# A row of scores by two transfers through DRAM instead of four TensorE transposes, and three buffers used in place, in a fused graph network

## The chip, the cores and the metric

The kernel runs on one core of a Trainium2 chip. The metric is the device time of one launch in microseconds (us), from the first to the last instruction, median of the runs. A separate execution is recorded by the hardware profiler: every instruction of the five engines with its start and length, every DMA packet, and the semaphore events between them. TensorE is called PE in the profile (PEld is its weight load), VectorE DVE, ScalarE ACT, GpSimd POOL, SyncE SP.

## The reference

A batch of 128 graphs of 128 nodes with 256 features goes through four layers. Each is `x = layernorm(x + layer(x, adj))`. Layer 0 is a gated graph network, layers 1 to 3 are graph attention (GAT).

```python
# layer 0: three steps
A = (adj != 0)
for i in range(3):
    m = einsum('bnd,de->bne', h, weight[i])
    aggr = einsum('bst,bsd->btd', A, m)
    h = gru_cell(aggr, h, w_ih, w_hh, b_ih, b_hh)
# layers 1 to 3, each with its own W and a
Wh = einsum('bnf,of->bno', x, W)
f_i, f_j = Wh @ a1, Wh @ a2
e = leaky_relu(f_i[:, :, None] + f_j[:, None, :], 0.2)
e = where(adj == 0, very_negative, e)
h_prime = einsum('bij,bjo->bio', softmax(e), Wh)
```

The score of an edge from i to j needs f_i, one number for each partition (node i), and f_j, one number for each column (node j). The numbers f_j come out one per partition, so they have to become a row, and the same row has to stand on all 128 partitions.

## The kernel before

The 128 graphs are 32 groups of G = 4. All arithmetic is in float32. For each group `gru` does the three steps of layer 0 and `gat` the three attention layers. All groups are recorded first as a list of operations, each with its reads, its writes, the engines that could run it and a cost in nanoseconds. The class `Plan` then plays this list through once, at build time, and from it comes the order of instructions on every engine; there is no other scheduler. On the chip each engine runs its own queue strictly in that order, and semaphores enforce the dependencies.

What the planner knows:

- priorities: older groups go first; the last four groups (`LAST = 4`, the tail) get priorities by stage instead, so that their layers run side by side;
- pools of buffers (`pools`): `k2` and `k4` are the SBUF work tiles of 512 and 1024 floats per partition, `bank` and `gate` are the PSUM banks (3 and 5), `fx` takes the unused product of a score, `v` the columns of statistics. `own` keeps some buffers back for the oldest group. An operation starts only if a buffer is free;
- a latency from the end of an operation on one engine to the start of its successor on another, and a margin of 500 ns more where the successor runs on PE:

```python
LATENCY = {"PE": 250, "ACT": 220, "DVE": 200, "POOL": 250, "SP": 4000}
...
when = max([t + (margin + self.LATENCY[e2] if e2 != e else 0 if e == "PE" else 60) for e2, t in o.at.items()],
```

Here `e2` is the engine of the predecessor, which ended at `t`, and `e` that of the operation itself. Transfers are operations of SP of 60 ns, and their landing time is SP's latency. The argument `lag` adds to the latency of one operation. `port=BOTH` tells the planner that DVE and POOL must not run two such operations at the same time.

In `gru`, the adjacency of a group is loaded as integers into a tile of the pool `adj` (L479) and turned into a mask `am` of floats (L483). At the end of layer 0 this mask is turned into zeros and a very negative number (L570), which `gat` adds to the scores. The products of the gates are done with a Strassen scheme: the matmuls on L446, the copies out of PSUM on L506, L510, L513 (ACT) and the additions on L451 (DVE). The input x is loaded a second time for the residual (L569).

In `gat`, per layer and group:

1. L605, DVE: eight products with a sum, four for f_j (h = 1) and then four for f_i (h = 0); the sums go to the tile `f`, the products to `fx`;
2. L614, PE: four transposes of the column f_j, broadcast along the free dimension, against the identity; the bank then has the row f_j on all partitions, for each of the four graphs;
3. L619, DVE: four operations that add the mask to this row, write the result to `e_` and take the maximum over j;
4. L623, ACT: Prelu with f_i as bias; L632 and L636, DVE: the maximum after the leaky ReLU; L640, ACT: Exp with the sum;
5. L647 to L674: transposes of the softmax, its product with x, then the product with W;
6. L680, DVE: division by the sum and addition of x, into `y`; then `layernorm(y, total, xn)`, which writes a new tile `xn`: Square with a sum on ACT (L389), whose squares go into `xn` too and are overwritten later, small steps on DVE and POOL, and the scaling on ACT (L402).

Of the kernel before, what the change touches and what calls it, by code (L numbers as in the profile page):

```python
# [8 lines left out]
F32 = mybir.dt.float32  # L9
I32 = mybir.dt.int32  # L10
AF = mybir.ActivationFunctionType
ALU = mybir.AluOpType
AX = mybir.AxisListType

P = 128
D = 256
KC = D // P
G = 4
# [5 lines left out]
FAR = -5.0 * 2.0 ** 97  # L24
# [23 lines left out]
class Plan:  # L48
# [2 lines left out]

    LATENCY = {"PE": 250, "ACT": 220, "DVE": 200, "POOL": 250, "SP": 4000}

    MARGIN = 500

# [140 lines left out]
def adj_resnorm_kernel(  # L198
# [14 lines left out]
    nc = tc.nc  # L213
    B = x.shape[0]
    NG = B // G
    LAST = 4

    consts = ctx.enter_context(tc.tile_pool(name="consts", bufs=1))
    work = ctx.enter_context(tc.tile_pool(name="work", bufs=1))
    psum = ctx.enter_context(tc.tile_pool(name="psum", bufs=1, space=bass.MemoryType.PSUM))  # L220


    pools = {"gru": 4, "xs": 2, "adj": 2, "am": 5, "k2": 26, "k4": 19, "fx": 2, "f": 3, "mv": 4, "st": 6, "v": 16,
             "gate": 5, "bank": 3}
    own = ({"k2": 8, "k4": 5, "gate": 2, "v": 5, "fx": 0, "st": 0}, {"k2": 4, "k4": 2, "v": 5, "fx": 0, "st": 0})
    floats = {"gru": 0, "k4": 1024, "xs": 1024, "fx": 256, "f": 8, "mv": 8, "st": 6, "v": 4}
    tags = {t: (n, floats.get(t, 512)) for t, n in pools.items()}
    BOTH = ("DVE", "POOL")
    plan = Plan({t: n for t, (n, _) in tags.items()}, own)
    slots = {t: [(psum if t in ("gate", "bank") else work).tile([P, w], I32 if t == "adj" else F32, name=f"{t}{i}")  # L230
                 for i in range(n)] for t, (n, w) in tags.items() if w}

    def T(b):
        if b.at is None:
            width = 1
            for s in b.shape:
                width *= s
            at = slots[b.tag][b.slot][:, 0:width]
            if len(b.shape) == 2:
                at = at.rearrange("p (a b) -> p a b", b=b.shape[-1])  # L240
            elif len(b.shape) == 3:
                at = at.rearrange("p (a b c) -> p a b c", b=b.shape[-2], c=b.shape[-1])
            b.at = at
        return b.at

    def bank():
        return Buf("bank", GN)
# [7 lines left out]
    ident = consts.tile([P, P], F32)  # L255
# [111 lines left out]
            res.append(dst)  # L367
        return res

    def layernorm(y, total, dst, prio):  # L370

        rstd, ve, shift = Buf("v", G), Buf("v", G), Buf("v", G)
        if total is None:
            mv = Buf("mv", G, 2)
            for b in range(G):
                st = Buf("st", 6)
                plan.op({"DVE": 400}, lambda e, b=b, st=st: nc.vector.bn_stats(T(st), T(y)[:, b, :]),
                        reads=[(y, b)], writes=[st], prio=prio)
                plan.op({"DVE": 95}, lambda e, b=b, st=st: nc.vector.bn_aggr(T(mv)[:, b, :], T(st)),
                        reads=[st], writes=[(mv, b)], prio=prio)  # L380
            plan.op({"POOL": 229}, lambda e: nc.gpsimd.tensor_scalar(T(ve), T(mv)[:, :, 1], EPS, None, op0=ALU.add),
                    reads=[(mv, b) for b in range(G)], writes=[ve], prio=prio)
            less, keys = (lambda: T(mv)[:, :, 0]), [(mv, b) for b in range(G)]
        else:
            mean, ss = Buf("v", G), Buf("v", G)
            plan.op({"DVE": 100}, lambda e: nc.vector.tensor_scalar(T(mean), T(total), -1.0 / D, None, op0=ALU.mult),  # L386
                    reads=[(total, b) for b in range(G)], writes=[mean], prio=prio)
            for b in range(G):
                plan.op({"ACT": 490}, lambda e, b=b: nc.scalar.activation(  # L389
                    T(dst)[:, b, :], T(y)[:, b, :], AF.Square, bias=T(mean)[:, b:b + 1], accum_out=T(ss)[:, b:b + 1]),  # L390
                    reads=[(y, b), mean], writes=[(dst, b), (ss, b)], prio=prio)
            plan.op({"POOL": 229}, lambda e: nc.gpsimd.tensor_scalar(  # L392
                T(ve), T(ss), 1.0 / D, EPS, op0=ALU.mult, op1=ALU.add),
                reads=[(ss, b) for b in range(G)], writes=[ve], prio=prio)
            less, keys = (lambda: T(mean)), [mean]
        plan.op({"POOL": 1035}, lambda e: nc.gpsimd.tensor_tensor(T(rstd), T(ve), neghalf, ALU.pow),
                reads=[ve], writes=[rstd], prio=prio)
        plan.op({"DVE": 100}, lambda e: nc.vector.scalar_tensor_tensor(  # L398
            T(shift), less(), -1.0 if total is None else 1.0, T(rstd), op0=ALU.mult, op1=ALU.mult),
            reads=keys + [rstd], writes=[shift], prio=prio)  # L400
        for b in range(G):
            plan.op({"ACT": 500}, lambda e, b=b: nc.scalar.activation(  # L402
                T(dst)[:, b, :], T(y)[:, b, :], AF.Identity, bias=T(shift)[:, b:b + 1], scale=T(rstd)[:, b:b + 1]),
                reads=[(y, b), shift, rstd], writes=[(dst, b)], prio=prio)

    def sums(ms, prio):

# [63 lines left out]

    def gru(g, stage):

        xs, adj_i, am = Buf("xs", G, D), Buf("adj", G, P), Buf("am", G, P)
        prio = stage(g, 0)
        turn = Buf("gru")
        x_g = x[g * G:(g + 1) * G].rearrange("b n d -> n b d")
        plan.op({"SP": 60}, lambda e: nc.sync.dma_start(T(xs), x_g), writes=[xs], prio=prio)
        plan.op({"SP": 60}, lambda e: nc.sync.dma_start(T(adj_i), adj[g * G:(g + 1) * G].rearrange("b s t -> s b t")),  # L479
                writes=[adj_i], prio=prio)  # L480
        if g == 0:
            hidden_weights(prio)
        plan.op({"DVE": 417}, lambda e: nc.vector.tensor_scalar(T(am), T(adj_i), 0, None, op0=ALU.not_equal),  # L483
                reads=[adj_i], writes=[am, turn], prio=prio, port=BOTH)
        hT = transposed(xs, lambda b, c: T(xs)[:, b, c * P:(c + 1) * P], prio)
        h = None
        for i in range(STEPS):
            prio = stage(g, i)
            if g == 0:
                input_weights(i, prio)  # L490
            agg = []
            for c in range(KC):
                b_, a_ = bank(), Buf("k2", GN)
# [23 lines left out]
            nn = strassen([(2, (h_in,)), (2, (a_in,))], halves, prio)  # L517
            hT2 = []
            for c in range(KC):

                o, v, d = rz[c], nn[c], Buf("k2", GN)
# [4 lines left out]
                for gt in range(2):  # L526
                    if c == 0:
                        plan.op({"ACT": 630}, lambda e, gt=gt, o=o, tanh=tanh: tanh(gt, 0, GN, lambda: T(o)[:, gt, :]),
                                reads=[(o, 0), (o, 1)], writes=[(o, 2 + gt)], prio=prio)
                    else:  # L530
                        plan.op({"ACT": 365}, lambda e, gt=gt, tanh=tanh, rz=rz: tanh(
                            gt, 0, H, lambda: T(rz[2])[:, gt * H:(gt + 1) * H]),
                            reads=[rz[2]], writes=[(o, 4 + gt)], prio=prio)
                        plan.op({"ACT": 400}, lambda e, gt=gt, o=o, tanh=tanh: tanh(gt, H, GN, lambda: T(o)[:, gt, H:GN]),
                                reads=[(o, 1), (o, 4 + gt)], writes=[(o, 2 + gt)], prio=prio)
                if c == 1:
                    plan.op({"ACT": 370}, lambda e, v=v, nn=nn: nc.scalar.activation(
                        T(v)[:, 0, 0:H], T(nn[2])[:, 0:H], AF.Identity, bias=bhn[:, 1:2]),
                        reads=[nn[2]], writes=[(v, 0)], prio=prio)
# [26 lines left out]
                hT2.append(d)  # L566
            if last:
                y = Buf("k4", G, D)
                plan.op({"SP": 60}, lambda e: nc.sync.dma_start(T(y), x_g), reads=[agg[0]], writes=[y], prio=prio)  # L569
                plan.op({"DVE": 417}, lambda e: nc.vector.tensor_scalar(  # L570
                    T(am), T(am), 0.0, FAR, op0=ALU.is_equal, op1=ALU.mult), reads=[am], writes=[am], prio=prio, port=BOTH)
            else:
                h2 = [Buf("k2", G, P) for c in range(KC)]
# [14 lines left out]
                        e, T(h2[c]), T(b_).rearrange("p (b d) -> p b d", b=G)), reads=[b_], writes=[h2[c]], prio=prio)  # L588
            if not last:
                h, hT = h2, hT2  # L590
        x1 = Buf("k4", G, D)
        layernorm(y, None, x1, prio)
        return x1, am

    def gat(g, xc, no, stage):

        for l in range(3):
# [9 lines left out]
                        accum_out=T(f)[:, b, h:h + 1]), reads=[(xc, b), (wa, l)], writes=[fx, (f, 2 * b + h)], prio=prio, port=BOTH)  # L607
            e_, pT, y = Buf("k2", G, P), Buf("k2", G, P), Buf("k4", G, D)
            top, nmax, den, rden, total = Buf("v", G), Buf("v", G), Buf("v", G), Buf("v", G), Buf("v", G)
            b_ = bank()  # L610

            def fn(e, b_=b_, f=f):
                for b in range(G):
                    nc.tensor.transpose(T(b_)[:, b * P:(b + 1) * P],  # L614
                                        T(f)[:, b, 1:2].to_broadcast([P, P]), ident)
            plan.op({"PE": 440}, fn, reads=[(f, 2 * b + 1) for b in range(G)], writes=[b_], prio=prio)

            for b in range(G):
                plan.op({"DVE": 215}, lambda e, b_=b_, b=b, e_=e_, top=top: nc.vector.tensor_tensor_reduce(  # L619
                    T(e_)[:, b, :], T(b_)[:, b * P:(b + 1) * P], T(no)[:, b, :], 1.0, 3 * FAR, ALU.add, ALU.max,  # L620
                    T(top)[:, b:b + 1]), reads=[b_, no], writes=[(e_, b), (top, b)], prio=prio)
            for b in range(G):
                plan.op({"ACT": 285}, lambda e, b=b, f=f, e_=e_: nc.scalar.activation(  # L623
                    T(e_)[:, b, :], T(e_)[:, b, :], AF.Prelu, bias=T(f)[:, b, 0:1], alpha=SLOPE),
# [43 lines left out]
            for b0 in range(0, G, 2):  # L668
# [9 lines left out]
                for b in (b0, b0 + 1):  # L678
# [2 lines left out]
                                T(y)[:, b, :], T(b_)[:, (b - b0) * D:(b - b0 + 1) * D], T(rden)[:, b:b + 1],  # L681
                                T(xc)[:, b, :], op0=ALU.mult, op1=ALU.add, accum_out=T(total)[:, b:b + 1]),
                            reads=[b_, rden, (xc, b)], writes=[(y, b), (total, b)], prio=prio)
            xn = Buf("k4", G, D)
            layernorm(y, total, xn, prio)
            xc = xn
        plan.op({"SP": 60}, lambda e: nc.sync.dma_start(out[g * G:(g + 1) * G].rearrange("b n d -> n b d"), T(xc)),
                reads=[(xc, b) for b in range(G)], prio=prio)

# [54 lines left out]
```

## Time and profile before

| what | value |
|---|---|
| time, median of 3 runs | 2719.54 us (2718.88 to 2719.57) |
| span of the profiled execution | 2716.7 us |
| granted TensorE clock | 0.998 |
| L614, transposes of f_j: number, median record | 384, 273 ns |
| L619, row plus mask: number, median record | 384, 284 ns |
| L605, products for f: number, median record | 768, 420 ns |
| L446, matmuls of the gates: number of records, median record | 8064, 379 ns |
| transfer of x for one group, issue to landing | 3.9 us (512 KB) |
| transfer of adj for one group, issue to landing | 2.9 us (256 KB) |
| transfer of the output of one group, issue to landing | 3.0 us (512 KB) |

A record is the time from an instruction's start to its end. Instructions of one engine overlap with the next in its pipeline, so the distance from start to start is shorter. A line of the timeline has the start, the length (of all that it merges), engine, source line, operation, tiles and how many; in brackets stands how long the engine was idle before and which instruction ended that. Busy time of an engine counts the union of its records.

### The profile page before, as it was taken

To read this page: it belongs to the slowest core of one execution; us is meant where nothing else is said; L and a number is where in the kernel's file an instruction comes from. 1 tells how busy PE (TensorE), PEld (TensorE's weight loads), DVE (VectorE), ACT (ScalarE), POOL (GpSimd) and SP (SyncE) were. 2 spreads that over 40 slices of the span, in tenths; PEclk is the share of its full clock that TensorE was granted. 3 is DMA by queue.
4 is the path that set the end of the run, shared out by engine and by line. 5 is a ranking of instruction groups with operands and counts; after the bars stand their busy time and mean duration, and the time that the engine had idled before them with its cause. 6 is when DMAs were issued, how large, how long until landed. Compare 5 with 4: busy or idle time off the path is not lost.

```text
span 2716.7 us, 42471 instructions
## 1 busy us (share of the span) xinstructions
PE 2660.0 (98%) x14536; PEld 2366.2 (87%) x14536; DVE 2026.1 (75%) x6206; ACT 1760.2 (65%) x4632; POOL 593.0 (22%) x738
## 2 busy tenths in 40 slices
PE   7999999999999999999999999999999999999987
PEld 6888889888888888888888888988988888888875
DVE  4677777787787776777876777877777877776696
ACT  3566666666666666666767666666676666665577
POOL 1013222211131222122221222212222312222021
PEclk9999999999999999999999999999999999999999
DMA  3001000000010100001000000100000000000000
GB/s 120 9 20 36 28 5 24 28 28 20 13 33 12 36 20 20 16 20 36 20 28 28 9 28 20 36 20 20 17 20 28 28 24 21 9 9 27 13 1 32
DMA packets 70106, 65.39 MB, mean 24 GB/s; under 512 B 2688, under 2 KB 68224, under 8 KB 69888
## 3 DMA queue, kind: packets, MB, share of 16 engines
q1 hardware_dynamic: 67584, 58.73, 7.1%
q10 hardware_dynamic: 2304, 3.95, 0.4%
q8 instruction: 114, 1.87, 0.3%
q14 instruction: 104, 0.85, 0.1%
HBM read 45.89 MB, written 16.78 MB: 23 GB/s over the span
## 4 chain that ended last, share of the span: by engine, by line
PE 86%; DVE 8%; ACT 3%; issue 1%; DMA 1%; POOL 0%; POOLq 0%; ACTq 0%; SPq 0%; DVEq 0%
PE gate L446 58%; PE bank L674 10%; PE bank L663 6%; PE bank L498 5%; PE bank L579 3%; DVE fx L605 2%; PE bank L647 1%; DVE k L451 1%; PE bank L614 1%; ACT k L402 1%; ACT k L389 1%; DVE k L680 1%; DVE k L286 1%; PE bank L333 1%; DVE k L540 1%
## 5 line engine op out<-in xcount | busy, mean ns | idle before, releaser
L446 PE MATMUL gate<-k,whs 128*128 128x256 f32 x4032 | 1202.2, 380 | 3.0 <-ACT k L513 2.2
L446 PE MATMUL gate<-k,wcs 128*128 128x256 f32 x4032 | 1199.2, 379 | 0.0
L446 PEld LDWEIGHTS gate<-k,wcs 128*128 128x128 f32 x4032 | 766.1, 190 | 104.0
L446 PEld LDWEIGHTS gate<-k,whs 128*128 128x128 f32 x4032 | 728.5, 190 | 86.2 <-ACT k L513 3.4
L451 DVE TENSOR_TENSOR k<-gate,k 128x512 f32<-128x512 f32 x576 | 390.4, 686 | 264.3 <-PE gate L446 220.9
L284 ACT COPY k<-bank 128x512 f32<-128x512 f32 (+1 forms) x459 | 262.3, 583 | 191.7 <-PE bank L579 62.7
L674 PE MATMUL bank<-gwT,k 128*128 128x256 f32 x1536 | 352.6, 382 | 5.0 <-DVE k L286 3.5
L416 POOL TENSOR_TENSOR k<-k,k 128x256 f32<-128x256 f32 x302 | 248.9, 841 | 402.0 <-DVE k L563 133.9
L674 PEld LDWEIGHTS bank<-gwT,k 128*128 128x128 f32 x1536 | 290.6, 191 | 49.7 <-DVE k L286 8.6
L605 DVE SCALAR_TENSOR_TENSOR fx<-k,wa 128x256 f32<-128x256 f32 x768 | 290.3, 436 | 51.2 <-ACT k L402 49.4
L389 ACT ACTIVATE k<-k,v 128x256 f32<-128x256 f32 x384 | 190.3, 498 | 210.6 <-DVE v L386 210.2
L402 ACT ACTIVATE k<-k,v,v 128x256 f32<-128x256 f32 x512 | 263.7, 593 | 54.7 <-DVE v L398 54.4
L524 ACT ACTIVATE k<-k,brz 128x512 f32<-128x512 f32 (+1 forms) x384 | 226.1, 619 | 80.6 <-DVE k L451 80.2
L680 DVE SCALAR_TENSOR_TENSOR k<-bank,v,k 128x256 f32<-128x256 f32 x384 | 169.9, 480 | 119.9 <-PE bank L674 119.3
L506 ACT COPY k<-gate 128x512 f32<-128x512 f32 x288 | 164.7, 580 | 109.8 <-PE gate L446 108.6
L553 ACT ACTIVATE k<-k,bi 128x512 f32<-128x512 f32 x192 | 137.8, 722 | 108.5 <-DVE k L550 71.1
L663 PEld LDWEIGHTS bank<-k,k 128*128 128x128 f32 x1536 | 185.9, 192 | 14.2 <-DVE k L286 5.3
L663 PE MATMUL bank<-k,k 128*128 128x128 f32 x1536 | 188.2, 275 | 7.8 <-DVE k L286 4.7
L558 POOL TENSOR_TENSOR k<-k,k 128x512 f32<-128x512 f32 x78 | 103.3, 1327 | 412.3 <-ACT k L553 406.1
L286 DVE COPY k<-bank 128x512 f32<-128x512 f32 x225 | 152.9, 685 | 49.3 <-PE bank L579 17.4
L392 POOL TENSOR_SCALAR v<-v 128x4 f32<-128x4 f32 x96 | 20.5, 214 | 773.4 <-ACT k L389 749.9
L510 ACT ACTIVATE k<-gate,bhn 128x256 f32<-128x256 f32 x288 | 135.5, 470 | 46.7 <-PE gate L446 45.9
(79 smaller groups left out, 3116.0 us busy)
## 6 DMA issues: line engine op xcount, KB each, us to landing
xs<-in_x_dram SPq DMA_DIRECT2D x32, 512.0 KB, 3.9
k<-in_x_dram SPq DMA_DIRECT2D x32, 512.0 KB, 4.0
out_dram<-k SPq DMA_DIRECT2D x32, 512.0 KB, 3.0
adj<-in_adj_dram SPq DMA_DIRECT2D x32, 256.0 KB, 2.9
k<-in_w_hhT_dram ACTq DMA_DIRECT2D x2, 384.0 KB, 6.6
k<-in_w_ihT_dram ACTq DMA_DIRECT2D x2, 384.0 KB, 6.5
k<-in_gnn_wT_dram ACTq DMA_DIRECT2D x3, 256.0 KB, 5.6
k<-in_gat_w_dram ACTq DMA_DIRECT2D x3, 256.0 KB, 5.2
```

What stands on the lines that cost most here:

```text
L284: nc.scalar.copy(dst, src)
L286: nc.vector.tensor_copy(dst, src)
L389: plan.op({"ACT": 490}, lambda e, b=b: nc.scalar.activation(T(dst)[:, b, :], T(y)[:, b, :], AF.Square, bias=T(mean)[:, b:b + 1], accum_out ...
L402: plan.op({"ACT": 500}, lambda e, b=b: nc.scalar.activation(T(dst)[:, b, :], T(y)[:, b, :], AF.Identity, bias=T(shift)[:, b:b + 1], scale= ...
L416: nc.vector if e == "DVE" else nc.gpsimd).tensor_tensor(T(t)[:, j, :], a(), b(), ALU.subtract),
L446: nc.tensor.matmul(T(dst)[:, j * H:(j + 1) * H], T(w)[:, m, gt, :], moving(m, ms)[1](), start=first and n == 0, stop=n == len(todo) - 1, s ...
L451: plan.op({"DVE": 630}, lambda e: nc.vector.tensor_add(T(o)[:, :, j * H:(j + 1) * H], T(b_).rearrange("p (g n) -> p g n", g=2), T(part).re ...
L524: nc.scalar.activation(T(o)[:, gt, n0:n1], src(), AF.Tanh, bias=brz[:, gt * KC + c:gt * KC + c + 1], scale=0.5)
L605: plan.op({"DVE": 345}, lambda e, b=b, h=h, l=l, f=f, fx=fx, xc=xc: nc.vector.scalar_tensor_tensor(T(fx), T(xc)[:, b, :], 1.0, T(wa)[:, l, ...
L663: nc.tensor.matmul(T(b_)[:, b * P:(b + 1) * P], T(xc)[:, b, c * P:(c + 1) * P], T(pT)[:, b, :], start=True, stop=True)
L674: nc.tensor.matmul(T(b_)[:, (b - b0) * D:(b - b0 + 1) * D], T(aT[k])[:, b * P:(b + 1) * P], T(gwT)[:, l, k, :], start=(k == 0), stop=(k == ...
L680: nc.vector.scalar_tensor_tensor(T(y)[:, b, :], T(b_)[:, (b - b0) * D:(b - b0 + 1) * D], T(rden)[:, b:b + 1], T(xc)[:, b, :], op0=ALU.mult ...
```

## The change

For the groups outside the tail, the column f_j is written from SBUF to a small DRAM tile of 4 x 128 floats, element by element, and read back from there as one row of 512 floats to all partitions, straight into `e_`. The operation that adds the mask then works on `e_` in place, and takes both inputs from SBUF. The four transposes and the PSUM bank between them are gone in these 28 groups; the tail keeps them. What it is for: TensorE has less to do, and one use of the three banks less in each layer.

Three edits save buffers: adj is loaded straight into the mask's tile and converted in place, which removes the pool `adj`; LayerNorm scales `y` in place, with the squares in a scratch tile `jx`; and `fx` has one tile instead of two. The pool `k2` gets one tile more. SP's latency is 2500 ns instead of 4000, with `lag` making up for it at the loads of x (1500) and adj (500). The residual load of x waits for a tanh of the last step (`(nn[0], 5)`) where it waited for the first aggregation.

```diff
-    LATENCY = {"PE": 250, "ACT": 220, "DVE": 200, "POOL": 250, "SP": 4000}
+    LATENCY = {"PE": 250, "ACT": 220, "DVE": 200, "POOL": 250, "SP": 2500}
...
-    pools = {"gru": 4, "xs": 2, "adj": 2, "am": 5, "k2": 26, "k4": 19, "fx": 2, "f": 3, "mv": 4, "st": 6, "v": 16,
+    pools = {"gru": 4, "xs": 2, "am": 5, "k2": 27, "k4": 19, "fx": 1, "jx": 1, "f": 3, "row": 3, "mv": 4, "st": 6, "v": 16,
...
+    slots["row"] = [dram.tile([G, P], F32, name=f"row{i}") for i in range(pools["row"])]
...
             for b in range(G):
-                plan.op({"ACT": 490}, lambda e, b=b: nc.scalar.activation(
-                    T(dst)[:, b, :], T(y)[:, b, :], AF.Square, bias=T(mean)[:, b:b + 1], accum_out=T(ss)[:, b:b + 1]),
-                    reads=[(y, b), mean], writes=[(dst, b), (ss, b)], prio=prio)
+                jx = Buf("jx", D)
+                plan.op({"ACT": 490}, lambda e, b=b, jx=jx: nc.scalar.activation(
+                    T(jx), T(y)[:, b, :], AF.Square, bias=T(mean)[:, b:b + 1], accum_out=T(ss)[:, b:b + 1]),
+                    reads=[(y, b), mean], writes=[jx, (ss, b)], prio=prio)
...
-        xs, adj_i, am = Buf("xs", G, D), Buf("adj", G, P), Buf("am", G, P)
+        xs, am = Buf("xs", G, D), Buf("am", G, P)
...
-                plan.op({"SP": 60}, lambda e: nc.sync.dma_start(T(y), x_g), reads=[agg[0]], writes=[y], prio=prio)
+                plan.op({"SP": 60}, lambda e: nc.sync.dma_start(T(y), x_g), reads=[(nn[0], 5)], writes=[y], prio=prio, lag=1500)
...
+            if g < NG - LAST:
+                row = Buf("row", P)
+                plan.op({"SP": 60}, lambda e, row=row, f=f: nc.sync.dma_start(
+                    slots["row"][row.slot].rearrange("b n -> n b"), T(f)[:, :, 1]),
+                    reads=[(f, 2 * b + 1) for b in range(G)], writes=[row], prio=prio)
+                plan.op({"SP": 60}, lambda e, row=row, e_=e_: nc.sync.dma_start(
+                    T(e_).rearrange("p b j -> p (b j)"),
+                    slots["row"][row.slot].rearrange("b n -> (b n)").partition_broadcast(P)),
+                    reads=[row], writes=[(e_, b) for b in range(G)], prio=prio)
+                rows, keys, port = (lambda b, e_=e_: T(e_)[:, b, :]), lambda b: [], BOTH
+            else:
...
             for b in range(G):
-                plan.op({"DVE": 215}, lambda e, b_=b_, b=b, e_=e_, top=top: nc.vector.tensor_tensor_reduce(
-                    T(e_)[:, b, :], T(b_)[:, b * P:(b + 1) * P], T(no)[:, b, :], 1.0, 3 * FAR, ALU.add, ALU.max,
-                    T(top)[:, b:b + 1]), reads=[b_, no], writes=[(e_, b), (top, b)], prio=prio)
+                plan.op({"DVE": 215}, lambda e, rows=rows, b=b, e_=e_, top=top: nc.vector.tensor_tensor_reduce(
+                    T(e_)[:, b, :], rows(b), T(no)[:, b, :], 1.0, 3 * FAR, ALU.add, ALU.max,
+                    T(top)[:, b:b + 1]), reads=keys(b) + [no, (e_, b)], writes=[(e_, b), (top, b)], prio=prio, port=port)
```

In the changed kernel some lines have new numbers: L446 is L449, L451 is L454, L605 is L607, L619 is L634, L623 is L638, L640 is L655, L680 is L695. The two transfers are issued on L615 and L618.

More of the change, by code (lines that the diff above doesn't have):

```diff
@@ L219, in adj_resnorm_kernel @@
     work = ctx.enter_context(tc.tile_pool(name="work", bufs=1))
+    dram = ctx.enter_context(tc.tile_pool(name="dram", bufs=1, space=bass.MemoryType.DRAM))
     psum = ctx.enter_context(tc.tile_pool(name="psum", bufs=1, space=bass.MemoryType.PSUM))
-    pools = {"gru": 4, "xs": 2, "adj": 2, "am": 5, "k2": 26, "k4": 19, "fx": 2, "f": 3, "mv": 4, "st": 6, "v": 16,
+    pools = {"gru": 4, "xs": 2, "am": 5, "k2": 27, "k4": 19, "fx": 1, "jx": 1, "f": 3, "row": 3, "mv": 4, "st": 6, "v": 16,
              "gate": 5, "bank": 3}
-    own = ({"k2": 8, "k4": 5, "gate": 2, "v": 5, "fx": 0, "st": 0}, {"k2": 4, "k4": 2, "v": 5, "fx": 0, "st": 0})
-    floats = {"gru": 0, "k4": 1024, "xs": 1024, "fx": 256, "f": 8, "mv": 8, "st": 6, "v": 4}
+    own = ({"k2": 8, "k4": 5, "gate": 2, "v": 5, "fx": 0, "jx": 0, "st": 0}, {"k2": 4, "k4": 2, "v": 5, "fx": 0, "jx": 0, "st": 0})
+    floats = {"gru": 0, "k4": 1024, "xs": 1024, "fx": 256, "jx": 256, "f": 8, "mv": 8, "st": 6, "v": 4}
     tags = {t: (n, floats.get(t, 512)) for t, n in pools.items()}
@@ L229, in adj_resnorm_kernel @@
     plan = Plan({t: n for t, (n, _) in tags.items()}, own)
-    slots = {t: [(psum if t in ("gate", "bank") else work).tile([P, w], I32 if t == "adj" else F32, name=f"{t}{i}")
-                 for i in range(n)] for t, (n, w) in tags.items() if w}
+    slots = {t: [(psum if t in ("gate", "bank") else work).tile([P, w], F32, name=f"{t}{i}")
+                 for i in range(n)] for t, (n, w) in tags.items() if w and t != "row"}
+    slots["row"] = [dram.tile([G, P], F32, name=f"row{i}") for i in range(pools["row"])]
     def T(b):
@@ L368, in transposed, with layernorm @@
         return res
-    def layernorm(y, total, dst, prio):
+    def layernorm(y, total, prio):
         rstd, ve, shift = Buf("v", G), Buf("v", G), Buf("v", G)
@@ L402, in layernorm @@
             plan.op({"ACT": 500}, lambda e, b=b: nc.scalar.activation(
-                T(dst)[:, b, :], T(y)[:, b, :], AF.Identity, bias=T(shift)[:, b:b + 1], scale=T(rstd)[:, b:b + 1]),
-                reads=[(y, b), shift, rstd], writes=[(dst, b)], prio=prio)
+                T(y)[:, b, :], T(y)[:, b, :], AF.Identity, bias=T(shift)[:, b:b + 1], scale=T(rstd)[:, b:b + 1]),
+                reads=[(y, b), shift, rstd], writes=[(y, b)], prio=prio)
     def sums(ms, prio):
@@ L477, in gru @@
         x_g = x[g * G:(g + 1) * G].rearrange("b n d -> n b d")
-        plan.op({"SP": 60}, lambda e: nc.sync.dma_start(T(xs), x_g), writes=[xs], prio=prio)
-        plan.op({"SP": 60}, lambda e: nc.sync.dma_start(T(adj_i), adj[g * G:(g + 1) * G].rearrange("b s t -> s b t")),
-                writes=[adj_i], prio=prio)
+        plan.op({"SP": 60}, lambda e: nc.sync.dma_start(T(xs), x_g), writes=[xs], prio=prio, lag=1500)
+        plan.op({"SP": 60}, lambda e: nc.sync.dma_start(T(am).bitcast(I32), adj[g * G:(g + 1) * G].rearrange("b s t -> s b t")),
+                writes=[am], prio=prio, lag=500)
         if g == 0:
             hidden_weights(prio)
-        plan.op({"DVE": 417}, lambda e: nc.vector.tensor_scalar(T(am), T(adj_i), 0, None, op0=ALU.not_equal),
-                reads=[adj_i], writes=[am, turn], prio=prio, port=BOTH)
+        plan.op({"DVE": 417}, lambda e: nc.vector.tensor_scalar(T(am), T(am).bitcast(I32), 0, None, op0=ALU.not_equal),
+                reads=[am], writes=[am, turn], prio=prio, port=BOTH)
         hT = transposed(xs, lambda b, c: T(xs)[:, b, c * P:(c + 1) * P], prio)
@@ L590, in gru @@
                 h, hT = h2, hT2
-        x1 = Buf("k4", G, D)
-        layernorm(y, None, x1, prio)
-        return x1, am
+        layernorm(y, None, prio)
+        return y, am
     def gat(g, xc, no, stage):
@@ L609, in gat, with fn @@
             top, nmax, den, rden, total = Buf("v", G), Buf("v", G), Buf("v", G), Buf("v", G), Buf("v", G)
[L610 to L616, printed above, removed]
+            if g < NG - LAST:
[9 more added lines that the diff above has]
+            else:
+                b_ = bank()
+                def fn(e, b_=b_, f=f):
+                    for b in range(G):
+                        nc.tensor.transpose(T(b_)[:, b * P:(b + 1) * P],
+                                            T(f)[:, b, 1:2].to_broadcast([P, P]), ident)
+                plan.op({"PE": 440}, fn, reads=[(f, 2 * b + 1) for b in range(G)], writes=[b_], prio=prio)
+                rows, keys, port = (lambda b, b_=b_: T(b_)[:, b * P:(b + 1) * P]), lambda b, b_=b_: [b_], ("POOL",)
@@ L683, in gat @@
                             reads=[b_, rden, (xc, b)], writes=[(y, b), (total, b)], prio=prio)
-            xn = Buf("k4", G, D)
-            layernorm(y, total, xn, prio)
-            xc = xn
+            layernorm(y, total, prio)
+            xc = y
         plan.op({"SP": 60}, lambda e: nc.sync.dma_start(out[g * G:(g + 1) * G].rearrange("b n d -> n b d"), T(xc)),
```

## The prediction

> **What bounds the kernel now.** I read the page's first parts, then the busy times by stretch, then the chain of waits, and last a timeline around one use of the operations concerned. From the page, busy time of each engine:
>
> ```profile
> PE 2660.0 (98%) x14536; PEld 2366.2 (87%) x14536; DVE 2026.1 (75%) x6206; ACT 1760.2 (65%) x4632; POOL 593.0 (22%) x738
> ```
>
> By stretch (span; busy time of PE, PEld, DVE, ACT, POOL; clock; DMA share; GB/s):
>
> ```profile
> 68.00:2600.00 2532.00, 2517.85 (x13797) 2249.85 (x13797) 1903.82 (x5680) 1640.59 (x4275) 563.58 (x693) 1.00 0.07 22
> 0.00:68.00 68.00, 51.81 (x230) 41.69 (x231) 30.17 (x61) 25.47 (x52) 9.06 (x15) 1.00 0.38 120
> 2600.00:2717.00 117.00, 90.33 (x512) 74.68 (x510) 92.11 (x466) 94.10 (x308) 20.39 (x30) 0.96 0.06 19
> ```
>
> In the 2532 us between head and tail TensorE idles 14 us: no other engine can hold it up for long now, and every TensorE instruction that disappears there is worth its full time. DVE has 628 us of idle time there. The chain that ended last, merged:
>
> ```profile
> 1003.65 0.44 PE bank L364 x4
> 1004.09 0.89 PE bank L498 x8
> 1004.98 0.44 PE bank L614 x4
> 1005.42 5.18 PE gate L446 x24
> ```
>
> It runs through TensorE instruction by instruction, and the four transposes of f_j (L614) cost 0.44 us of it, 0.108 each, though a record says 274 ns: matmuls overlap.
>
> TensorE is full because the planner's order arrives on time. One use shows how tight that is (start, length, engine, line):
>
> ```profile
> 1116.14 0.60 PE L614 MATMUL bank<-ident,f 128*128 128x128 f32 x4
> ...
> 1116.26 0.76 DVE L416 TENSOR_TENSOR k<-k,k 128x256 f32<-128x256 f32 x2
> ...
> 1116.93 0.28 DVE L619 CUSTOM_DVE_ANT_0 k<-bank,am 128x128 f32<-128x128 f32 x1
> ...
> 1117.26 1.28 ACT L623 ACTIVATE k<-k,f 128x128 f32<-128x128 f32 x4 [0.33 <-DVE v L619]
> ...
> 1118.51 0.59 ACT L506 COPY k<-gate 128x512 f32<-128x512 f32 x1
> ...
> 1120.04 0.59 PE L446 MATMUL gate<-k,whs 128*128 128x256 f32 x2
> ```
>
> L619 feeds the Prelu (L623) on ACT; behind that, in ACT's queue, stands the GRU's gate copy L506 (to 1119.10), and the matmuls at 1120.04 need its bank. So a DVE late by more than about 0.9 us at L619 stops TensorE, through work of another group.
>
> **What the Trainium skill says.** "DMA: Bandwidth & Descriptors", section "Latency and other measured facts", puts the fixed cost of a transfer at about 2 us, mostly the receipt. Before's smallest main-loop transfers agree in kind: adj 2.9 us and the output 3.0 us to landing. The same page, "Two DMAs through the same engine are not ordered": a transfer that reads what another wrote must wait for its semaphore. So the two landings add up; no pair of before's transfers shows this. Its section "Rules for kernel authors" says that a last dimension with a stride becomes one descriptor per element: the write of the row is 512 descriptors of 4 bytes. No transfer of before has that form. "SBUF — State Buffer", section "Who interferes with whom": a DVE operation with two SBUF inputs and a GpSimd one that reads SBUF block each other. L619 gets two SBUF inputs; POOL is busy 22%, and before has no row that shows the price.
>
> **The change, part by part.** *Removed:* in 28 of 32 groups, 3 layers each, the four transposes: 84 x 4 x 0.108 = 36.4 us of TensorE, all on the path. One use of the three PSUM banks per layer goes too; with 14 us of idle time it can bring little more.
>
> *Added, the two transfers.* The row needs both in turn. Write: 512 packets are 32 on each of 16 queues; the output's transfer starts its packets 0.9 us after its issue and lands 0.45 us after the last, by the trace's DMA records; a packet took 9 ns at 4 or 24 bytes and 27 ns at 512. So 0.9 + 32 x 0.009 to 0.027 + 0.45 = 1.6 to 2.2 us; small writes to DRAM may cost more, and I take 2.1, with 3.0 (the output's whole landing) as the upper end. Read with broadcast: 128 x 2 KB = 256 KB, as many bytes as adj, which landed in 2.9 us by the page; with a quarter of the packets I take 2.6 (2.2 to 2.9). Semaphores to SP, between the two and to DVE: 0.2 together, estimated from DVE's successors, which start 0.03 to 0.1 us after their releasers. Sum 4.9 us, bounds 4.2 and 5.6 for all but bad luck, 6.1 at the extreme.
>
> *What the plan allows for that.* The planner releases an operation at its predecessor's end plus the predecessor engine's latency, but plus 60 ns where both run on the same engine. The second transfer waits for the first on the same SP: so the plan has 200 + 60 + 60 + 60 + 2500 = 2880 ns from f_j to L634 (the new place of L619): one landing, not two. In the changed program's DVE order I counted, for all 84 uses, what stands between the fourth f_j and the first L634: four to eleven instructions, nearly always the four products of f_i (0.345 apart), the rest L454, L419, L288 and the GRU's elementwise lines. At before's start-to-start times, with f_j's own 0.43 and about 0.1 us for each product that now waits for the one ahead (fx has one buffer), the mean is 3.25 us (10th and 90th percentile 2.5 and 4.0). So L634 stands at the head of DVE's queue for 4.9 - 3.25 = 1.65 us on average, 139 us over 84 uses. Behind it in DVE's queue stand gate additions (L454) and evictions (L288) of the other group, which TensorE waits for to reuse banks; behind the Prelu in ACT's queue the gate copies, as above.
>
> *What of it reaches TensorE.* From before's trace, for each of the 84 first L619: how much later it could have run before a first TensorE instruction moves, following the in-order queues and the waits. Mean 1.19 us, median 1.10, 10th and 90th percentile 0.30 and 1.98. Taking every one of the 84 waits against every slack, and only the excess: 0.65 us per use, 54 us in all. With a chain of 4.2 us the same sum gives 21 us, with 4.55 it equals the 36 us saved, with 5.6 it gives 102, with 6.1 about 140. Each excess adds up, since the next f_j comes later by as much.
>
> *Edits at nothing.* adj loaded into the mask's buffer: same bytes, same L483 (0.42 us), hidden behind a group's lead. LayerNorm in place: the same instructions on ACT; it frees 1024 floats a layer, with no TensorE wait to remove. The loads of x and adj keep 4.0 and 3.0 us in the plan. Square into one buffer jx: four waits of ACT on itself, ACT is 65% busy. L634's first input from SBUF instead of PSUM: 0.21 us start to start, I take no difference; both ends of it (0.05 us x 4 x 84 = 17 us of DVE) lie in idle time. fx with one buffer: 768 products, up to 0.1 us each on DVE; in the tail, where DVE is 79% busy and the 12 uses keep their transposes, I put 3 us on the path (0 to 8).
>
> Sum: 2719.5 - 36.4 + 54 + 3 = 2740 us.
>
> **The rivals.** *A, the transfers stay hidden.* Chain of 4.2 us or less: 2719.5 - 36.4 + 21 = 2704; with no stop at all, 2683. For it: TensorE's saving is certain and DVE has 628 us idle; 4-byte packets of 9 ns would land early. Against: the plan counts one landing of the two. *B, a far worse chain.* 4-byte writes at the output's whole landing and waits in SP's in-order queue behind loads of other groups (each transfer of the row waits there): 6 us and more, 2719.5 - 36.4 + 133 to 140 = 2816 to 2825. For it: SP's queue now holds a blocked wait 84 times. Against: DMA is 7% busy. *C, the excess equals the saving:* 2720, needs a chain within some 0.1 us of 4.55. *D, the GAT chain becomes the bound:* a layer takes about 25 us from L619 to L619 and three layers a period of 81 us, so 4 us more per layer makes 87; the order may overlap groups, so I count this as part of B.
>
> **How the numbers follow.** Main forecast, a chain of 4.6 to 5.6: 0.41. A: 0.40, as the balance point is only 0.35 us under my estimate and the packet times leave room below. C: 0.06. B and D: 0.13. Slower is 0.54, faster 0.40. The range reaches from between A's two values to the middle of B: 2690 to 2800, with about 0.1 left out at each end.
>
> **What would show it.** Right: DVE waits of 100 to 200 us before L634 for the row's transfer; TensorE's idle time between head and tail at 14 + 54, its busy time 36 us less; landings of about 2.1 and 2.6 us. Wrong: L634 without waits (the plan's lead suffices), or long waits with TensorE still at 14 us idle (the slack is larger than counted), or landings over 3 us each (B).

## The result, and the profile after

The changed kernel takes 3629.86 us (median of 6 runs, 3622.94 to 3633.53) against 2719.45: a ratio of 1.3345, 95% interval 1.3328 to 1.3362. The direction was forecast, the size was not: 910 us more instead of 20.

The page of the changed kernel. First the busy times by engine and the granted clock in 40 slices, then the chain that ended last, the group of the mask operation, and the two transfers (last number: us from issue to landing):

```profile
PE 2835.8 (78%) x14200; PEld 2467.0 (68%) x14200; DVE 2063.7 (57%) x6314; ACT 1776.1 (49%) x4619; POOL 516.4 (14%) x643
...
PEclk9998888988988888888988888888989888899999
...
PE 47%; DMA 31%; DVE 10%; ACT 8%; issue 3%; POOL 0%; DVEq 0%; SPq 0%; POOLq 0%; ACTq 0%
PE gate L449 29%; DMA row<-f 21%; DMA k<-row 10%; PE bank L689 7%; PE bank L678 4%; DVE fx L607 4%; PE bank L501 3%; ACT k L405 2%; PE bank L662 2%; PE bank L582 2%; DVE k L634 2%; DVE k L454 1%; ACT k L638 1%; ACT jx L392 1%; ACT k L655 1%
...
L634 DVE CUSTOM_DVE_ANT_0 k<-k,am 128x128 f32<-128x128 f32 x336 | 80.8, 289 | 876.8 <-DMA k<-row 876.8
...
k<-row SPq DMA_DIRECT2D x84, 256.0 KB, 4.4
...
row<-f SPq DMA_DIRECT2D x84, 2.0 KB, 9.0
```

The same line of the chain in the kernel before:

```profile
PE 86%; DVE 8%; ACT 3%; issue 1%; DMA 1%; POOL 0%; POOLq 0%; ACTq 0%; SPq 0%; DVEq 0%
```

A chain that was PE for 86% is now DMA for 31%. DVE stands 876.8 us before L634, 10.4 us in each of the 84 uses. The write of 2 KB takes 9.0 us to land, the read 4.4. PE has 336 transposes fewer, yet its busy time has grown by 176 us.

One use, on DVE's timeline, on PE's, and then by stretch (span; busy time of PE, PEld, DVE, ACT, POOL; clock; DMA share; GB/s):

```profile
826.33 0.08 DVE L607 DVE_READ_ACCUMULATOR fx<-k,wa 128x1 f32 x1
836.82 0.29 DVE L634 CUSTOM_DVE_ANT_0 k<-k,am 128x128 f32<-128x128 f32 x1 [10.41 <-DMA k<-row]
```

```profile
830.25 0.59 PE L449 MATMUL gate<-k,wcs 128*128 128x256 f32 x2
839.00 1.63 PE L662 MATMUL bank<-ident,k 128*128 128x128 f32 x4 [8.15 <-ACT k L655]
840.42 1.06 PE L449 MATMUL gate<-k,whs 128*128 128x256 f32 x2
841.27 1.06 PE L449 MATMUL gate<-k,wcs 128*128 128x256 f32 x2
```

```profile
824.00:828.00 4.00, 4.00 (x20) 3.54 (x19) 2.41 (x10) 0.71 (x2) 0.00 (x0) 1.00 0.07 1
828.00:832.00 4.00, 2.85 (x14) 2.16 (x12) 0.00 (x0) 0.00 (x0) 0.00 (x0) 1.00 0.00 0
832.00:836.00 4.00, 0.00 (x0) 0.00 (x0) 0.00 (x0) 0.00 (x0) 0.00 (x0) 0.62 0.31 51
836.00:838.00 2.00, 0.00 (x0) 0.00 (x0) 1.18 (x11) 0.85 (x3) 0.00 (x0) 0.50 0.10 29
838.00:840.00 2.00, 1.00 (x3) 0.55 (x3) 2.00 (x7) 1.98 (x10) 0.33 (x2) 0.50 0.44 131
840.00:842.00 2.00, 2.00 (x6) 1.58 (x6) 1.64 (x6) 1.43 (x5) 0.93 (x1) 0.50 0.02 4
842.00:844.00 2.00, 2.00 (x10) 1.68 (x10) 1.10 (x6) 2.00 (x5) 0.00 (x0) 0.70 0.00 0
844.00:846.00 2.00, 2.00 (x18) 1.92 (x17) 1.39 (x4) 1.18 (x3) 0.00 (x0) 1.00 0.00 0
```

DVE stops at 826.4, PE runs dry four microseconds later. While it stands, the granted clock falls to half and stays there after PE has begun again: two matmul records take 1.06 us at 840.42, where they took 0.59 before. The Trainium skill describes this ("TensorE: Matmul & The Clock Gate", Part 1: a clock gate halves the rate after an idle window of about 3.4 us and gives it back after as long a busy one). For long pauses the trace agrees: all 84 of PE's pauses of over 6 us between head and tail are followed by a stretch at 0.5; there are 88 such stretches, 842 us in all, against 2 with 12 us before.

The extra time then has two parts. PE's pauses are 776 us against 41: 735 more. Its busy time is 2835.8 against 2660.0, and 36 of the latter are gone: 212 more. 735 + 212 - 36 = 911, and the spans differ by 912 (3629.1 - 2716.7). That these add up is no proof, since a span is its busy time and its pauses. But in the stretches at 0.5 PE is busy for 400 us, of which full speed would have saved half: 200 of the 212 us are the slow clock.

### The profile page after: what moved, and what is told of

It reads as the page before. It is cut to its first block, busy times and chain, and to the rows that moved or that the text cites. A ratio compares the mean times of both kernels' runs of the same rounds, so it can differ in the third digit from the quotient of the medians.

```text
span 3629.1 us, 42135 instructions
## 1 busy us (share of the span) xinstructions
PE 2835.8 (78%) x14200; PEld 2467.0 (68%) x14200; DVE 2063.7 (57%) x6314; ACT 1776.1 (49%) x4619; POOL 516.4 (14%) x643
## 4 chain that ended last, share of the span: by engine, by line
PE 47%; DMA 31%; DVE 10%; ACT 8%; issue 3%; POOL 0%; DVEq 0%; SPq 0%; POOLq 0%; ACTq 0%
PE gate L449 29%; DMA row<-f 21%; DMA k<-row 10%; PE bank L689 7%; PE bank L678 4%; DVE fx L607 4%; PE bank L501 3%; ACT k L405 2%; PE bank L662 2%; PE bank L582 2%; DVE k L634 2%; DVE k L454 1%; ACT k L638 1%; ACT jx L392 1%; ACT k L655 1%
## 5 line engine op out<-in xcount | busy, mean ns | idle before, releaser
L449 PE MATMUL gate<-k,whs 128*128 128x256 f32 x4032 | 1287.5, 403 | 387.0 <-DVE k L454 209.2
L449 PE MATMUL gate<-k,wcs 128*128 128x256 f32 x4032 | 1261.1, 396 | 0.0
L449 PEld LDWEIGHTS gate<-k,whs 128*128 128x128 f32 x4032 | 777.8, 203 | 502.1 <-DVE k L454 209.8
L449 PEld LDWEIGHTS gate<-k,wcs 128*128 128x128 f32 x4032 | 811.7, 201 | 125.0
L634 DVE CUSTOM_DVE_ANT_0 k<-k,am 128x128 f32<-128x128 f32 x336 | 80.8, 289 | 876.8 <-DMA k<-row 876.8
L638 ACT ACTIVATE k<-k,f 128x128 f32<-128x128 f32 x384 | 127.7, 391 | 911.2 <-DVE v L634 911.0
L454 DVE TENSOR_TENSOR k<-gate,k 128x512 f32<-128x512 f32 x576 | 390.7, 685 | 234.8 <-PE gate L449 194.5
L607 DVE SCALAR_TENSOR_TENSOR fx<-k,wa 128x256 f32<-128x256 f32 x768 | 337.4, 439 | 33.9 <-ACT k L405 16.7
L662 PE MATMUL bank<-ident,k 128*128 128x128 f32 x384 | 100.1, 375 | 224.5 <-ACT k L655 214.9
L695 DVE SCALAR_TENSOR_TENSOR k<-bank,v,k 128x256 f32<-128x256 f32 x384 | 169.8, 480 | 138.5 <-PE bank L689 137.9
L392 ACT ACTIVATE jx<-k,v 128x256 f32<-128x256 f32 x384 | 194.4, 506 | 109.0 <-DVE v L388 105.0
L662 PEld LDWEIGHTS bank<-ident,k 128*128 128x128 f32 x384 | 65.8, 181 | 264.1 <-ACT k L655 244.1
L419 POOL TENSOR_TENSOR k<-k,k 128x256 f32<-128x256 f32 x208 | 172.5, 842 | 455.8 <-ACT k L286 152.9
```

The lines of the kernel that those rows point to most:

```text
L392: plan.op({"ACT": 490}, lambda e, b=b, jx=jx: nc.scalar.activation(T(jx), T(y)[:, b, :], AF.Square, bias=T(mean)[:, b:b + 1], accum_out=T( ...
L419: nc.vector if e == "DVE" else nc.gpsimd).tensor_tensor(T(t)[:, j, :], a(), b(), ALU.subtract),
L449: nc.tensor.matmul(T(dst)[:, j * H:(j + 1) * H], T(w)[:, m, gt, :], moving(m, ms)[1](), start=first and n == 0, stop=n == len(todo) - 1, s ...
L454: plan.op({"DVE": 630}, lambda e: nc.vector.tensor_add(T(o)[:, :, j * H:(j + 1) * H], T(b_).rearrange("p (g n) -> p g n", g=2), T(part).re ...
L607: plan.op({"DVE": 345}, lambda e, b=b, h=h, l=l, f=f, fx=fx, xc=xc: nc.vector.scalar_tensor_tensor(T(fx), T(xc)[:, b, :], 1.0, T(wa)[:, l, ...
L662: nc.tensor.transpose(T(b_)[:, b * P:(b + 1) * P], T(e_)[:, b, :], ident)
```

## The experiments

**Transposes back.** Theory: the two transfers alone cost the time. Edit:

```diff
-            if g < NG - LAST:
+            if g < 0:
```

> The changed kernel with the four transposes in all 32 groups, all other edits kept (adj, mask and LayerNorm in place, one fx, jx, the lags). Theory 1 (the row's two transfers alone cost the time: DVE waits 877 us for them): 2710 to 2730 us, no DVE wait for a row, clock near 1.0. Rival (the in-place edits and the single fx buffer add waits of their own): over 2750 us, with more idle TensorE time in the middle.

Measured: 2728.85 us, ratio 1.0036 (1.0022 to 1.005), no wait for a row, clock 0.996. Without the transfers 901 of the 910 us are gone, and the rival falls. The other edits as they stand are not free, though: 9.8 us.

**The transfers by themselves.** At the end of the kernel before, 40 transfers, each waiting for the one ahead, four rounds of:

```diff
+            nc.sync.dma_start(d1.rearrange("b n -> n b"), pq[:, :, 1])                        # L710
+            nc.sync.dma_start(pd, d1.rearrange("b n -> (b n)").partition_broadcast(P))        # L711
+            nc.sync.dma_start(d2, pm)                                                         # L712
+            nc.sync.dma_start(pd, d2.rearrange("n b -> (n b)").partition_broadcast(P))        # L713
+            nc.sync.dma_start(d1, pr)                                                         # L714
+            nc.sync.dma_start(pd, gat_w[:, 0].rearrange("p k d -> p (k d)"))                  # L715
+            nc.sync.dma_start(d3[:, :, 0].rearrange("b n -> n b"), pq[:, :, 1])               # L716
+            nc.sync.dma_start(pm, d3[:, :, 0].rearrange("b n -> n b"))                        # L717
+            nc.sync.dma_start(d4[:, :, 0].rearrange("b n -> n b"), pq[:, :, 1])               # L718
+            nc.sync.dma_start(pm, d4[:, :, 0].rearrange("b n -> n b"))                        # L719
```

> The kernel before, with 40 more transfers on SP at its end, each waiting for the one ahead: the row's write as in the change (512 pieces of 4 bytes side by side in 2 KB of DRAM), its broadcast read (128 x 2 KB from one row), a write of 128 pieces of 16 bytes, its broadcast read, a write of 4 pieces of 512 bytes, a read of 128 different rows of 2 KB, and writes of 512 pieces of 4 bytes 64 and 512 bytes apart, each read back by pieces of 4 bytes. The time of the whole is about 200 us over before and says nothing. Theory 1a (the landing of the write grows with the number of pieces that share a line of DRAM): 8 to 10 us as in the change, 3 us or less for 16 bytes and for 512 bytes, and 4 bytes set apart also 3 us or less. Rival 1b (it grows with the number of pieces wherever they go): 8 to 10 us for all three forms with 512 pieces. Rival 1c (the landing in the change came from other traffic): about 2.5 us for every form here. For the reads: 4.4 us for the broadcast against under 3 us for different rows if the one row is what slows it; equal if not.

The run took 120 us longer than the kernel before, not 200. One round on SP's timeline (start of the issue, its length). As each waits for the one ahead, the distance to the next line is the time to landing and about 0.02 us:

```profile
2745.46 0.36 SPq L710 DMA_DIRECT2D d<-k  x1
2754.77 0.33 SPq L711 DMA_DIRECT2D k<-d  x1
2759.13 0.33 SPq L712 DMA_DIRECT2D d<-k  x1
2760.56 0.32 SPq L713 DMA_DIRECT2D k<-d  x1
2764.68 0.26 SPq L714 DMA_DIRECT2D d<-k  x1
2765.86 0.34 SPq L715 DMA_DIRECT2D k<-in_gat_w_dram  x1
2768.50 0.37 SPq L716 DMA_DIRECT2D d<-k  x1
2770.72 0.37 SPq L717 DMA_DIRECT2D k<-d  x1
2772.70 0.36 SPq L718 DMA_DIRECT2D d<-k  x1
2774.73 0.36 SPq L719 DMA_DIRECT2D k<-d  x1
2776.61 0.36 SPq L710 DMA_DIRECT2D d<-k  x1
```

Landings over the four rounds:

| transfer of 2 KB, or read of 256 KB | us |
|---|---|
| L710 write, 512 pieces of 4 bytes side by side | 8.5 to 10.8 |
| L716 write, 512 pieces of 4 bytes, 64 bytes apart | 1.8 to 2.2 |
| L718 write, the same, 512 bytes apart | 1.7 to 2.0 |
| L712 write, 128 pieces of 16 bytes side by side | 1.4 to 2.1 |
| L714 write, 4 pieces of 512 bytes | 1.2 |
| L711, L713 read, one row of 2 KB to 128 partitions | 3.6 to 5.1 |
| L715 read, 128 different rows of 2 KB | 2.5 to 2.6 |

Rival 1b falls: the same 512 pieces 64 bytes apart land in 1.8 to 2.2 us. So does rival 1c: the write side by side takes 8.5 us and more with nothing else under way. What costs is 512 small pieces packed into the same 2 KB, which fits 1a. Steps between 4 and 64 bytes were not tried, so how close is too close stays open. In the trace's DMA records the packets of such a write, with nothing else under way, have all started after 1.3 us, at 7 to 9 ns each; the other 7 to 8 us pass before the landing is reported and show in no packet. What the memory does in that time was not observed. The broadcast read is slower too: 4.2 us (median) against 2.6 for as many bytes from different rows. But it also takes bytes that the transfer ahead has just written, and the read of L715 does not; which of the two makes it slower was not separated.

**Pieces of 16 bytes.** The same idea with f_j as four neighbouring floats per partition:

```diff
-            f = Buf("f", G, 2)
+            f = Buf("f", 2, G)
...
-                row = Buf("row", P)
+                row, er = Buf("row", P), Buf("er", P, G)
                 plan.op({"SP": 60}, lambda e, row=row, f=f: nc.sync.dma_start(
-                    slots["row"][row.slot].rearrange("b n -> n b"), T(f)[:, :, 1]),
+                    slots["row"][row.slot], T(f)[:, 1, :]),
...
-                    T(e_).rearrange("p b j -> p (b j)"),
-                    slots["row"][row.slot].rearrange("b n -> (b n)").partition_broadcast(P)),
+                    T(er).rearrange("p j b -> p (j b)"),
+                    slots["row"][row.slot].rearrange("n b -> (n b)").partition_broadcast(P)),
...
-                rows, keys, port = (lambda b, e_=e_: T(e_)[:, b, :]), lambda b: [], BOTH
+                rows, keys, port = (lambda b, er=er: T(er)[:, :, b]), lambda b, er=er: [er], BOTH
```

> The changed kernel with f_j kept as four neighbouring floats per partition, so that the write is 128 pieces of 16 bytes into a DRAM tile of 128 x 4; the row is read back as 2 KB into a tile of its own with the graphs interleaved, and L634 reads it with a step of 4 floats. One tile less in k2, two new tiles for it. The plan's latencies as in the change. Theory 1 with 1a or 1b: the write lands in 3 us or less, the chain is 7.5 to 8 us instead of 14, DVE's wait about 400 us, time about 3000 to 3150 us. Rival 1c: no change in the landing, time about 3630 us.

Measured: 2925.78 us in one run. The write lands in 1.4 us, the read in 4.0 (medians). What DVE waits for, longest first (us in total, times, longest):

```profile
DVE k L634 <- DMA er<-row: 223.7, 83, 5.8
DVE k L454 <- PE gate L449: 141.6, 131, 8.7
```

The chain came out shorter than expected (5.9 us on average from f_j to the landing of the read, not 7.5 to 8; 13.6 in the changed kernel), and wait and time fell below the ranges given. With the chain 8 us shorter 704 us are back, and still 206 us are lost. The plan still counts 2.9 us, and whether that is the reason is tested below.

This trace also shows that short pauses can bring the half clock:

```profile
189.07 1.18 PE L449 MATMUL gate<-k,whs 128*128 128x256 f32 x2 [2.84 <-ACT k L509]
190.03 1.06 PE L449 MATMUL gate<-k,wcs 128*128 128x256 f32 x2
```

After a pause of 2.84 us two matmul records take 1.06 us again. Of the 26 stretches at 0.5 that begin between head and tail, 19 have no pause of over 3 us in the 3.4 us ahead of them; so the idle window of about 3.4 us that "TensorE: Matmul & The Clock Gate" (Part 1) states is no safe limit for a single pause here. In all, PE is busy for 120 us at half clock here, some 60 us lost.

**The plan told.** The changed kernel as it is, with `lag=9000` on the write and `lag=2000` on the read.

> The changed kernel with the planner told what the transfers take: lag 9000 ns for the write and 2000 more for the read, nothing else. Theory 1 (the order was wrong, because the plan allowed 2.9 us where 14 pass; the latency itself can be filled with another group's work): DVE's wait falls from 877 to under 150 us, the clock back over 0.97, time 2700 to 2800 us. Rival 2 (three attention layers of a group, each 11 us longer, no longer fit beside one period of 81 us, so latency bounds the kernel in any order): over 3000 us, with TensorE idle in long pieces.

Measured: 2913.76 us, ratio 1.0717 (1.0701 to 1.0733), clock 0.962. Rival 2 falls: the same long chain costs a net 195 us, not 910, when the order allows for it. But theory 1's range is missed by over 100, and DVE's wait and the clock are just outside theirs. Two lines of the waits, of DVE and of PE:

```profile
DVE k L634 <- DMA k<-row: 159.6, 38, 15.0
```

```profile
PE bank L366 <- DMA xs<-in_x_dram: 61.0, 10, 11.9
```

Here the landings of the write spread from 8.5 to 15.4 us (in the 21 of 84 uses for which the trace tells the landing), and the first load of x keeps PE waiting. So a longer allowance, 13000 and 3000:

> The changed kernel's write in pieces of 4 bytes, with the planner told 13000 ns for the write and 5500 for the read (9000 and 4500 gave 2914 us, with 160 us of DVE waits, landings of the write of 8.5 to 15.4 us and 61 us of TensorE waits for x). If the scatter of the landings was what remained: DVE's wait under 60 us and 2740 to 2830 us. If the other loads, stuck in SP's queue and behind the small pieces, are the larger part: 2850 to 2950 us, with TensorE's waits for x at 60 us or more.

Measured: 2901.44 us, ratio 1.0666 (1.0646 to 1.0686). The second range holds. DVE's wait is still 103 us and PE's wait for x stays at 61. The second load of x lands after 13.9 us, against 4.0 in the kernel before; but this is the median of the only four of 32 loads for which the trace tells the landing. A longer allowance brings 12 us. PE's pauses are 151 us longer than before, and 56 of these are waits for x; what makes up the others, the waits for the row among them, was not separated, nor whether the loads are held up in SP's order or behind the small pieces in the DMA queues.

**Both.** The write in pieces of 16 bytes, with `lag=1700` and `lag=2200`:

> The kernel with the write in pieces of 16 bytes, and the planner told its landings: lag 1700 for the write (1.4 us measured), 2200 more than SP's 2500 for the read (4.0 us measured). Theory 1 (what cost the time was the landing that the plan did not count; once counted, other groups' work fills it, and TensorE keeps the 36 us of transposes): DVE's wait for the row under 30 us, clock over 0.99, time 2685 to 2715 us, under the kernel before. Rival 2 (the longer chain of the attention layers costs TensorE time in any order): 2730 us or more with hardly any DVE wait for the row. Rival 3 (the landings scatter too much for a fixed allowance): DVE's wait over 60 us and 2720 to 2800 us.

Measured: 2702.92 us, ratio 0.9936 (0.9922 to 0.995), clock 0.994. Waits of DVE for the row:

```profile
DVE k L634 <- DMA er<-row: 13.0, 12, 3.6
```

From 224 us in 83 waits to 13 us in 12, by two numbers in the plan and no other edit: the landings that the plan did not count were the reason. This is faster than both kernels, by 16.5 us against before. Against before, PE's busy time is 27 us lower (2633.2), not 36, and its pauses are 11 us longer (52). The gain is not that of the transposes alone, since the other edits are in it too.

**The edits in place.** Transposes in all groups, with two `fx` tiles and 26 in `k2`:

> The changed kernel with the transposes in all groups, as in the run that cost 0.36 per cent, but with two fx tiles and 26 k2 tiles as before. If the 10 us come from the one fx tile (each product waits for the end of the one ahead): 2717 to 2722 us. If from the other edits (jx, LayerNorm in place, the later load of the residual, the other order they lead to): 2726 us or more.

Measured: 2708.69 us, ratio 0.9956 (0.9944 to 0.9969), below both ranges. The second `fx` tile, for one in `k2`, brings 20 us, and the remaining edits gain 11 us on the kernel before; which of them does was not separated. So the transposes are nearly as good: this kernel is only 5.8 us slower than the 16-byte kernel with the plan told (2702.92), and 11 of the latter's 16.5 us can be had without any transfer of the row. With one tile a product that directly follows another starts 470 ns after it (median), with two 346. And the planner, which frees a buffer only 200 ns after its use, puts other work between: the eight products of a layer take 6.0 us instead of 2.85 (median, outside the tail).

**All of it together.** Two `fx` tiles in the 16-byte kernel, once for a tile of `k2` and once for a tile of `er`:

> The 16-byte kernel with the plan told, with two fx tiles and 25 k2 tiles (26 before it). If the one fx tile costs here what it cost with the transposes (20 us): 2680 to 2690 us. If the tile that k2 gives up costs as much: 2695 to 2710 us.

> The same with 26 k2 tiles and a single tile for the row that comes back. If buffers do not matter: as the run beside it, 2680 to 2690 us. If the single tile makes the read wait for the last use of the one ahead: DVE waits for the row, over 2700 us.

Measured: 2706.01 us (0.995, 0.9937 to 0.9962) and 2713.41 us (0.9978, 0.9969 to 0.9986). Neither beats 2702.92, so the second `fx` tile's gain does not add to the others. In the first, either what `k2` gives up costs about as much, or the faster products gain nothing there; no run separates the two. The kernel with a single `er` tile is slower by 7 us, and not by waits for the row: DVE waits 21.5 us for it there, 26.4 in the other. Its cause stays open.

## Why the prediction was wrong

- *What bounds the kernel, and the saving.* The transposes' cost was right: 336 at 0.108 us. In the best version PE's busy time is 27 us lower, and about 7 of the other 9 us are the clock (18 us busy at half clock there, 3 before). That each transpose is "worth its full time" did not come out: against the best kernel with transposes the net is 5.8 us, since PE's pauses grow from 32 to 52 us.
- *What the plan allows (2880 ns, one landing of two).* Right. The elapsed time stood up as well: from the fourth f_j to the start of DVE's wait 3.2 us passed on average, 3.25 were forecast. The whole chain from f_j to L634 took 13.7 us on average (9.0 and 4.4 are the medians of its two landings), and what is left after 3.2 is the 10.4 us that DVE waited per use.
- *What of it reaches TensorE.* Right in kind and nearly in size. With the measured waits in place of the forecast ones, the same 84 slacks give an excess of 778 us in the changed kernel, where PE's pauses grew by 735. With waits of 10.4 us against slacks of 1.2 that is a weak test. The 16-byte kernel is a better one: 130 us, where the pauses are 138 us longer than with the transposes back (186 against 47).
- *Added, the two transfers.* This step failed. I wrote "I take 2.1, with 3.0 (the output's whole landing) as the upper end" for the write and "I take 2.6 (2.2 to 2.9)" for the read. They took 9.0 and 4.4. The write's estimate multiplied packets by packet times, and the packets did take 7 to 9 ns; but the landing comes 7 to 8 us after the last packet, as the transfers by themselves show. The output's landing of 3.0 us was no upper end either, since its pieces are 1 KB and not 4 bytes. For the read I took adj, whose rows are all different. No row of before had either form, so the upper end was not bounded by anything. With the measured waits, the forecast's own sum is 2719.5 - 36.4 + 778 + 3 = 3464 us: most of what was missing.
- *Not in the sum at all:* the half clock after a pause, some 200 of the 910 us. It is not confined to the far case. The 16-byte kernel, at 5.9 us, has a chain between the 5.6 and the 6.1 us for which the forecast's sum gives 2788 and 2826 us. It took 2926; some 60 of those 100 to 140 us are the half clock, the others were not separated. So the sum would have been short even with the right landings.
- *Edits at nothing.* Wrong by small amounts that partly cancel: 20 us for the single `fx` tile (I had 3), 11 us gained by the others (I had none). That L634 takes no longer with both inputs in SBUF was right: 287 ns against 284 (medians).
- *Rival B* named the right kind of trouble, a far worse chain, but priced "6 us and more" only up to 6.1 us (and by its own terms the upper value is 2823 us, not 2825).
- *Rival D* (the attention chain becomes the bound) was not what happened: with the allowance the same chain of landings costs a net 195 us, and with a chain of 5.9 us the kernel is faster than before, with PE's pauses 11 us longer.

## What to carry to other kernels

In these runs a write's landing could not be worked out from its packets: 512 pieces of 4 bytes side by side took about five times as long to land as the same pieces set apart, and six times as long as 128 pieces of 16 bytes in the same 2 KB. So let the column become 16 bytes per partition before it leaves, and measure the landing of a form that the kernel does not have yet. Where an order is written out ahead, a chain of two transfers must be counted as two landings; a wait at the head of an in-order queue holds up other work, and here two numbers in the plan turned 7.6% slower into 0.6% faster. Ask of every new wait whether it can stop TensorE: in the middle of the changed kernel every pause of over 6 us was paid for a second time at half clock, and in the 16-byte kernel pauses of under 3 us were too, though not all of them. And compare with the old way under the same other edits: most of the final gain did not need the transfers.

## What was not expected of the hardware

512 pieces of 4 bytes into 2 KB of DRAM land in 8.5 to 10.8 us, into 32 KB in 1.8 to 2.2. One row of 2 KB read to 128 partitions takes 3.6 to 5.1 us, 128 rows 2.5 to 2.6. TensorE's clock fell to half after single pauses of under 3 us, 2.84 in the case shown. The mask operation reading its row with a step of 16 bytes has records of 383 ns (median), 287 without the step.
